# A seven-product Strassen kernel: the sixth product is accumulated into the first PSUM bank

## The chip, the core and the metric

The kernel runs on one core of one Trainium2 chip. The metric is the device time of one execution in microseconds; lower is better. The kernel before takes 2892.92 us, the median of three runs (2892.66 to 2893.03).

## What is computed

The input x has 8 batches, 512 channels and 32 x 32 = 1024 tokens, in fp32. Two attention layers follow each other:

```
layer 0:  xn = layer_norm(x over channels)
          q, k, v = xn Wq', xn Wk', xn Wv'  (+ biases), 8 heads of 64
          out = softmax(q k' / 8) v          per head
          x1  = x + out Wo' + bo
layer 1:  h = group_norm(x1, 32 groups)
          q, k, v = 1x1 projections of h
          p = softmax(q k' / sqrt(512))      one head of 512 channels
          y = x1 + Wp (p v) + bp
```

## The kernel before

The kernel folds the query and key weights of layer 1 into one matrix ("a") and its value and output weights into another ("m"), so layer 1 has a projection qa, scores s, a value projection vm and an output product o. Every product of full matrices is done by a Strassen scheme with seven half-size products instead of eight. The head attention of layer 0 (scores at L805, values at L823) is done directly.

**A unit.** Class `Product` (L325) does one such multiplication for one slice r of the output. `STEPS` (L54) lists its seven products in order: which block or sum of blocks of the left operand, which of the right operand, into which PSUM accumulator (x, y or z), and whether the product opens the accumulator or adds to it. A method `step` (L366) issues the matmuls of one step on TensorE, then pops up to `pieces` entries of side work from a queue (`tick`, L312), then issues what follows on the other engines: a copy of x to SBUF on ScalarE (`copy`, L350, through a function `shift` of the product), or an add of a kept copy and a PSUM bank on VectorE (`out`, L344). Before the change this goes as follows:

| step | product | after it |
|---|---|---|
| 0 | 11 x 11 opens x | copy x to u(0,0) |
| 1 | 12 x 21 opens z | block (0,0) = u(0,0) + z |
| 2 | S2 x T2 adds to x | copy x to u(0,1) |
| 3 | S1 x T1 opens y | nothing |
| 4 | S3 x T3 adds to x | copy x to u(1,1); block (1,1) = u(1,1) + y |
| 5 | 22 x T4 opens z | (q, k, qa and out copy x again with the bias of row block 1); block (1,0) = that copy + z |
| 6 | S4 x 22 adds to y | block (0,1) = u(0,1) + y |

In q, k and qa the copy is an ACTIVATE with a bias (L475), in v, vm, s and o a plain COPY (L458), in the out product a VectorE instruction that adds bias and residual (L901). In s every finished block then gets an exponential in place (L943). In o each finished block is scaled, gets bias and residual, and is stored (L1033 to L1035).

**Where the work stands.** A batch has 18 units: two each (r = 0 and 1) for q, k, v, out, qa, vm and o, four for s; eight batches have 144. The units of most products are issued one after the other: all steps of r = 0, then all of r = 1. In qa, o and each half of s both units do their first two steps before the first does the rest. k of batches 1 to 7 is spread: its first unit stands ahead of the out product, the second is stepped between the parts of the group norm (L1236) and, for its step 6, among the steps of qa (`meanwhile`, L1230).

**PSUM.** `banks_of` (L412) gives the accumulators. y is a bank per unit, from a pool of two. x and z are tiles of two banks (128 x 1024 fp32) from a pool of three; in most products the two units share one tile of each, r choosing the half:

```
            if to == "y":
                return bank(f"y_{tag}_{r}")
            if shared is None or to in own:
                return wide_psum(f"{to}_{tag}_{r}")[:, :HB]
            if to not in shared:
                shared[to] = wide_psum(f"{to}_{tag}")
            return shared[to][:, ts(r, HB)]
```

The out product has an x of its own for each unit (`own="x"`), and k of batches 1 to 7 shares nothing (`apart`).

**Order.** The engines' order is that in which the program issues the instructions (`manual_schedule`, L1089). The tile framework adds the semaphore waits; it finds from the tiles which instruction has to wait for which. SP's queue carries the loads and stores, POOL's queue the folding of row sums.

Of the kernel before, what the change touches and what calls it, by code (L numbers as in the profile page):

```python
# [34 lines left out]
def group_matrix(nc, grp):  # L35
# [21 lines left out]
    ("S2", "T2", "x", False),  # L57
    ("S1", "T1", "y", True),
    ("S3", "T3", "x", False),
    ("22", "T4", "z", True),  # L60
    ("S4", "22", "y", False),
]
BLOCK_OF = {1: (0, 0), 4: (1, 1), 5: (1, 0), 6: (0, 1)}
LOADS_AT = {0: [(0, 0), (0, 1)], 2: [(1, 1)], 3: [(1, 0)]}
SLOTS = ["11", "12", "22", "S1", "S2", "S3", "S4"]


# [1 line left out]
def fast_path(ctx: ExitStack, tc: tile.TileContext, x: bass.AP, vecs: dict, weights: dict, out: bass.AP,  # L69
# [35 lines left out]
    def half_tile(name):  # L105
        return half.tile([P, HB], F32, tag="h", name=name)
# [218 lines left out]
    class Product:  # L325
# [16 lines left out]
            self.done = 0  # L342

        def out(self, i, k, u, ps):  # L344
            if self.in_place and (i, k) != (1, 1):
                self.own[i, k] = u
            nc.vector.tensor_add(self.dest(i, k), u, ps)  # L347
            self.behind.append((i, k))

        def copy(self, which):  # L350
            u = self.loaded.pop(which) if which in self.loaded else half_tile(f"u{which}_{self.tag}")
            self.shift(u, self.x, which)
            return u

        def open(self, to, opens):
            if opens and not hasattr(self, to):
# [9 lines left out]
        def step(self, n=1):  # L366
            for _ in range(n):
                i = self.done
                self.done += 1
                a, b, to, opens = STEPS[i]  # L370
                until(lambda: a in self.a and b in self.b)
                self.open(to, opens)
                if self.ahead:
                    self.ahead(i)
                if i in self.led:
                    self.part(getattr(self, to), self.a[a], self.b[b], opens, (1,))
                elif i == 6 and self.last:
                    next(self.last)
                    return
                else:  # L380
                    self.part(getattr(self, to), self.a[a], self.b[b], opens)
                tick(self.pieces)
                if i == 0:
                    self.u1 = self.copy((0, 0))
                elif i == 1:
                    self.out(0, 0, self.u1, self.z)
                elif i == 2:
                    self.u2 = self.copy((0, 1))
                    if self.last:
                        next(self.last)  # L390
                elif i == 4:
                    u3 = self.copy((1, 1))
                    self.out(1, 1, u3, self.y)
                    self.u3 = u3
                elif i == 5:
                    if self.shift.twice:
                        self.u3 = self.copy((1, 0))
                    self.out(1, 0, self.u3, self.z)
                elif i == 6:
                    self.out(0, 1, self.u2, self.y)  # L400
                if i in (2, 4, 6) or self.at_once:
                    self.finish()

        def finish(self):
# [49 lines left out]
                                 stop=(m == NM // 2 - 1), skip_group_check=True)  # L454
        return part

    def plain_shift():
        return make_shift(lambda u, ps, which: nc.scalar.copy(u, ps))  # L458

    def make_shift(f, twice=False):  # L460
        f.twice = twice
        return f

    def project(tag, w, bias, h, apart=False):

        res, shared = {}, None if apart else {}

        def unit(r):
            def dest(i, k):
                if (i, k) not in res:  # L470
                    res[i, k] = block(f"{tag}_{i}{k}")
                return res[i, k][:, r, :]

            def shift(u, ps, which):
                nc.scalar.activation(u, ps, AF.Identity, bias=bias(2 * which[0] + r))  # L475

            return Product(f"{tag}_{r}", w, h, channel_part(r), make_shift(shift, True), dest,
                           banks_of(tag, r, shared))
        return [unit(r) for r in range(2)], res

    def project_v(tag, w, h):


        res, shared = {}, {}

        def unit(r):
            def dest(i, k):
                if (i, k) not in res:
                    res[i, k] = big_tile(f"{tag}_{i}{k}")
                return res[i, k][:, ts(r, HB)]  # L490

            return Product(f"{tag}_{r}", w, h, token_part(r), plain_shift(), dest, banks_of(tag, r, shared))
        return [unit(r) for r in range(2)], res

    def value_of(v, m, col, width):
# [384 lines left out]
    def project_out(b, w, ot, stats):  # L880

        x1 = {(i, k): block(f"x1_{b}_{i}{k}") for k in range(NH) for i in range(2)}
        shared = {}

        def unit(r):
            def dest(i, k):
                return x1[i, k][:, r, :]

            def load(which):
                i, k = which  # L890
                xr = u.loaded[which] = half_tile(f"xr_{b}_{k}_{2 * i + r}")
                nc.sync.dma_start(out=xr, in_=x[b, ts(2 * i + r, P), ts(k, HB)])

            def ahead(n):
                for which in LOADS_AT.get(n, []):
                    if which not in u.loaded:
                        load(which)

            def shift(t, ps, which):
                oc = 2 * which[0] + r  # L900
                nc.vector.scalar_tensor_tensor(t, ps, bo[:, oc : oc + 1], t, ALU.add, ALU.add)  # L901

            def after(i, k):
                later(lambda: nc.vector.bn_stats(stats[:, 2 * i + r, k, :], dest(i, k)))

            u = Product(f"out_{b}_{r}", w, ot, channel_part(r), make_shift(shift, True), dest,
                        banks_of(f"out_{b}", r, shared, own="x"), after)
            u.ahead = ahead
            load((0, 0))
            return u  # L910
        return [unit(r) for r in range(2)], x1


    class Whole:
# [14 lines left out]
        def scores(self):  # L929
            b = self.b  # L930
            shared = [{}, {}]

            def unit(r):
                g = r // 2

                def dest(i, k):
                    p = self.p[f"{k + 1}{i + 1}"]
                    if p[g] is None:
                        p[g] = block(f"p1_{b}_{k}{i}_{g}")
                    return p[g][:, r % 2, :]  # L940

                def after(i, k):
                    nc.scalar.activation(dest(i, k), dest(i, k), AF.Exp, scale=float(C) ** -0.5)  # L943

                return Product(f"s1_{b}_{r}", self.q, self.hb, key_part(r), plain_shift(), dest,
                               banks_of(f"s1_{b}_{g}", r % 2, shared[g]), after)

            return [unit(r) for r in range(4)]
# [62 lines left out]
        def values(self, v):  # L1011
# [4 lines left out]
            def unit(r):  # L1016
                y, xr_of = {}, {}

                def dest(i, k):
                    if (i, k) not in y:  # L1020
                        y[i, k] = half_tile(f"y_{b}_{r}_{i}{k}")
                    return y[i, k]
# [8 lines left out]
                def after(i, k):  # L1031
# [2 lines left out]
                    nc.vector.scalar_tensor_tensor(t, t, bm[:, oc : oc + 1], xr, ALU.add, ALU.add)  # L1034
                    nc.sync.dma_start(out=out[b, ts(oc, P), ts(k, HB)], in_=t)  # L1035

                u = Product(f"o1_{b}_{r}", w, self.p, value_part(r), plain_shift(), dest,
                            banks_of(f"o1_{b}", r, shared), after)
                def halves(u):


                    a, b_, to, opens = STEPS[6]
                    oc = r
                    xr = half_tile(f"x1r_{b}_last")
                    nc.sync.dma_start(out=xr, in_=self.x1[0, 1][:, ts(r, HB)])
                    nc.vector.tensor_mul(u.u2, u.u2, self.rden[:, ts(1, HB)])
                    nc.vector.scalar_tensor_tensor(xr, u.u2, bm[:, oc : oc + 1], xr, ALU.add, ALU.add)
                    t = dest(0, 1)
                    yield
                    both = (slice(0, HB // 2), slice(HB // 2, HB))  # L1050
                    for cols in both:
                        for m in range(NM // 2):
                            nc.tensor.matmul(u.y[:, cols], w[a][:, m, ts(r, P)],
                                             self.p[b_][m // 2][:, m % 2, cols], start=False,
                                             stop=(m == NM // 2 - 1), skip_group_check=True)
                    for cols in both:
                        queries = slice(HB + cols.start, HB + cols.stop)
                        nc.vector.tensor_mul(t[:, cols], u.y[:, cols], self.rden[:, queries])
                        nc.vector.tensor_add(t[:, cols], t[:, cols], xr[:, cols])
                        nc.sync.dma_start(out=out[b, ts(oc, P), queries], in_=t[:, cols])  # L1060
                    yield

                u.at_once = u.in_place = True
# [621 lines left out]
```

## Time and profile before

One profiled execution stands beside the three timed runs. The lines that the prediction quotes are not repeated here.

| what | value |
|---|---|
| median of three runs | 2892.92 us (2892.66 to 2893.03) |
| span of the profiled execution, first to last instruction | 2891.4 us; its time as a run is not recorded apart |
| median less span | 1.5 us |
| mean granted TensorE clock | 0.999 of full |
| ACTIVATE or COPY of x to SBUF, 128 x 512 | 687 ns (q, k, qa), 586 ns (v, vm, s, o) |
| add of a copy and a bank on VectorE, 128 x 512 | 684 to 689 ns |
| HBM traffic over the span | 79 GB/s |

How to read the rows: a timeline row has the start in us from the span's start, the length in us, engine, line, operation, output tile <- input tiles, shape, and how many instructions are merged in it; in brackets stands the idle time of the engine ahead of it and what ended that. A group row has the count, then busy us and mean ns of one, then idle time ahead and its cause. One fp32 matmul of the program shows as two records. A matmul's record is longer than the distance to the next, since they are pipelined: with 512 columns, 592 ns long and 429 ns apart. The names x_q, y_q, z_q are the accumulators of product q, u(i, k)_q the copies.

### The profile page before, as it was taken

Reading aid. Unit: us, or ns where it says so; the run is one execution under the profiler, and the core shown is the slowest. Engines: PE = TensorE matmul, PEld = TensorE weight load, DVE = VectorE, ACT = ScalarE, POOL = GpSimd, SP = SyncE. Lnnn points to the kernel's source line nnn. Section 1 sums busy time; section 2 is a strip of 40 time slices with the busy share of each in tenths; the row PEclk is TensorE's granted clock in tenths of the full one; section 3 lists DMA queues with packets and bytes.
Section 4 is the critical chain, followed back from the end, with each engine's and each line's share of the span. In section 5 each row is a group of like instructions: output and inputs, shape, how many; then the busy total and the mean of one; then the engine's idle time right before and its main releaser. Section 6 shows DMA issues by size and latency. Waiting matters only on the chain.

```text
span 2891.4 us, 27273 instructions
## 1 busy us (share of the span) xinstructions
PE 2875.6 (99%) x9695; PEld 1379.4 (48%) x9695; DVE 1790.3 (62%) x2325; ACT 1057.9 (37%) x1820; POOL 345.2 (12%) x507
## 2 busy tenths in 40 slices
PE   9999999999999999999999999999999999999999
PEld 4534455345553454534545345543455434553345
DVE  6668465774657655676556755568555685537844
ACT  4462314612256122651225512264222732226331
POOL 2020011200112011120111201011010110002000
PEclk9999999999999999999999999999999999999999
DMA  8134162341623326133252333433244231402302
GB/s 316 46 72 139 37 157 78 68 142 38 181 47 73 135 54 172 43 74 131 62 164 49 84 116 74 152 69 78 102 110 141 61 106 56 124 30 61 118 8 67
DMA packets 110129, 277.17 MB, mean 96 GB/s; under 512 B 16304, under 2 KB 20704, under 8 KB 109984
## 3 DMA queue, kind: packets, MB, share of 16 engines
q1 hardware_dynamic: 81760, 204.51, 20.3%
q0 software_dynamic: 28128, 70.81, 13.3%
q8 instruction: 78, 1.28, 0.2%
q14 instruction: 67, 0.55, 0.1%
q10 hardware_dynamic: 96, 0.02, 0.0%
HBM read 168.85 MB, written 59.24 MB: 79 GB/s over the span
## 4 chain that ended last, share of the span: by engine, by line
PE 97%; DVE 2%; ACT 0%; DMA 0%; issue 0%; DVEq 0%; SPq 0%; ACTq 0%
PE s L805 15%; PE acc L823 15%; PE x_o L453 6%; PE x_s L445 6%; PE y_s L445 4%; PE z_s L445 4%; PE z_o L453 4%; PE y_o L453 4%; PE x_v L437 3%; PE x_vm L437 3%; PE x_q L428 3%; PE x_qa L428 3%; PE x_out L428 3%; PE x_k L428 3%; PE y_q L428 2%; PE y_v L437 2%
## 5 line engine op out<-in xcount | busy, mean ns | idle before, releaser
L814 DVE TENSOR_TENSOR sum<-sum,p 128x1024 f32<-128x1024 f32 x384 | 470.4, 1225 | 40.1 <-DVE sum L814 1.4
L808 ACT ACTIVATE p<-s 128x1024 f32<-128x1024 f32 (+1 forms) x608 | 478.8, 984 | 42.7 <-PE s L805 42.7
L823 PE MATMUL acc<-p,v 128*64 128x512 f32 x2048 | 446.7, 594 | 0.0
L805 PE MATMUL s<-q,k_again 64*128 64x512 f32 x1792 | 392.1, 592 | 0.0
L823 PEld LDWEIGHTS acc<-p,v 128*64 128x64 f32 x2048 | 144.1, 137 | 298.6 <-issue 272.4
L805 PEld LDWEIGHTS s<-q,k_again 64*128 64x128 f32 x1792 | 170.7, 186 | 217.6 <-issue 136.0
L530 POOL DMA_DIRECT2D sum<-sum x78 | 64.0, 823 | 1722.3 <-PE z_vm L437 869.6
L526 POOL DMA_DIRECT2D fold<-sum x312 | 208.6, 755 | 329.4 <-DMA sum<-sum 201.4
L812 DVE TENSOR_TENSOR sum<-p,p 128x1024 f32<-128x1024 f32 x64 | 78.3, 1223 | 179.9 <-ACT p L808 179.9
L445 PE MATMUL x_s<-S_qa,T_gn 128*128 128x512 f32 x256 | 120.3, 592 | 0.0
L827 ACT COPY o<-acc 128x512 f32<-128x512 f32 x63 | 36.9, 586 | 220.0 <-PE acc L823 219.8
L453 PE MATMUL x_o<-T_p,S_vm 128*128 128x512 f32 x256 | 115.2, 592 | 0.0
L943 ACT ACTIVATE p<-p 128x512 f32<-128x512 f32 x128 | 80.7, 630 | 73.1 <-DVE p L347 73.0
L347 DVE TENSOR_TENSOR p<-u(1, 1)_s,y_s 128x512 f32<-128x512 f32 x32 | 22.0, 689 | 132.3 <-ACT u(1, 1)_s L458 132.3
L475 ACT ACTIVATE u(0, 0)_k<-x_k,vecs 128x512 f32<-128x512 f32 x16 | 11.0, 687 | 211.9 <-PE x_k L428 211.9
L869 ACT COPY rr<-r 32x16 f32<-32x16 f32 x256 | 52.6, 205 | 69.4 <-DVE r L772 66.1
L445 PEld LDWEIGHTS x_s<-S_qa,T_gn 128*128 128x128 f32 x256 | 48.6, 190 | 61.2 <-issue 61.0
L453 PEld LDWEIGHTS x_o<-T_p,S_vm 128*128 128x128 f32 x256 | 48.6, 190 | 60.8 <-issue 59.3
L347 DVE TENSOR_TENSOR y<-u(1, 1)_o,y_o 128x512 f32<-128x512 f32 x16 | 11.0, 687 | 99.0 <-ACT u(1, 1)_o L458 99.0
L901 DVE SCALAR_TENSOR_TENSOR xr<-x_out,bo,xr 128x512 f32<-128x512 f32 x64 | 47.7, 745 | 38.4 <-PE x_out L428 38.4
L520 DVE STREAM_TRANSPOSE rden<-rr 128x512 f32<-128x512 f32 (+1 forms) x72 | 53.3, 759 | 26.5 <-ACT rr L869 13.4
L347 DVE TENSOR_TENSOR qa<-u(1, 1)_qa,y_qa 128x512 f32<-128x512 f32 x16 | 11.0, 687 | 81.0 <-ACT u(1, 1)_qa L475 81.0
(353 smaller groups left out, 4589.3 us busy)
## 6 DMA issues: line engine op xcount, KB each, us to landing
sum<-sum POOLq DMA_DIRECT2D x78, 256.0 KB, 3.4
fold<-sum POOLq DMA_DIRECT2D x312, 64.0 KB, 2.4
x<-in_x_dram SPq DMA_DIRECT2D x32, 512.0 KB, 9.0
xr<-in_x_dram SPq DMA_DIRECT2D x64, 256.0 KB, 3.0
x_away<-x SPq DMA_DIRECT2D x32, 512.0 KB
x1r<-x_away SPq DMA_DIRECT2D x63, 256.0 KB, 3.3
k_away<-k SPq DMA_DIRECT2D x28, 512.0 KB, 2.6
k_again<-k_away SPq DMA_DIRECT2D x28, 512.0 KB, 5.5
```

The lines of the kernel that those rows point to most:

```text
L428: nc.tensor.matmul(dst, a[:, k, ts(r, P)], b[:, k, :], start=(opens and k == 0), stop=(k == 1), skip_group_check=True)
L437: nc.tensor.matmul(dst[:, ts(m, CB)], b[:, k, ts(2 * r + m, P)], a[:, k, :], start=(opens and m == 0 and k == 0), stop=(k == 1), skip_grou ...
L445: nc.tensor.matmul(dst, b[:, k, ts(r, P)], a[:, k, :], start=(opens and k == 0), stop=(k == 1), skip_group_check=True)
L453: nc.tensor.matmul(dst, a[:, m, ts(r, P)], b[m // 2][:, m % 2, :], start=(opens and m == 0), stop=(m == NM // 2 - 1), skip_group_check=True)
L526: nc.gpsimd.dma_start(out=f[ts(q + i, BL), :], in_=t[ts(n, BL), ts(i, HB)], accum_op=ALU.add if n else ALU.bypass)
L530: nc.gpsimd.dma_start(out=t[:D, :], in_=t[D:, :], accum_op=ALU.add)
L805: nc.tensor.matmul(parts[i], self.k[m // 4][r, ts(m % 4, P)], self.q[r, :], start=True, stop=True)
L808: nc.scalar.activation(dst, src, AF.Exp, scale=1.0 / float(D) ** 0.5)
L812: nc.vector.tensor_add(self.sum, self.p[0], p)
L814: nc.vector.tensor_add(self.sum, self.sum, p)
L823: nc.tensor.matmul(acc[i * D : (i + 1) * D, :], value_of(self.vt, m, self.c * P + i * D, D), self.p[m][:, ts(i, HB)], start=(m == 0), stop ...
L943: nc.scalar.activation(dest(i, k), dest(i, k), AF.Exp, scale=float(C) ** -0.5)
```

## The change

The sixth and seventh products change places, and 22 x T4 is added to x instead of opening z a second time. x then holds all of block (1,0) when the last step ends, and a single copy takes it out of PSUM: an ACTIVATE with bias in q, k and qa, a COPY in v, vm and o, an exponential straight from PSUM in s, and the bias-and-residual instruction in out. Block (1,1) is now made from a copy of y after step 3 and x after step 4. The loads of residuals follow the new order of blocks.

```diff
 STEPS:
     ("S2", "T2", "x", False),
     ("S1", "T1", "y", True),
     ("S3", "T3", "x", False),
-    ("22", "T4", "z", True),
     ("S4", "22", "y", False),
+    ("22", "T4", "x", False),
 ]
-BLOCK_OF = {1: (0, 0), 4: (1, 1), 5: (1, 0), 6: (0, 1)}
-LOADS_AT = {0: [(0, 0), (0, 1)], 2: [(1, 1)], 3: [(1, 0)]}
+BLOCK_OF = {1: (0, 0), 4: (1, 1), 5: (0, 1), 6: (1, 0)}
+LOADS_AT = {0: [(0, 0), (0, 1)], 1: [(1, 1)], 4: [(1, 0)]}
...
+        def whole(self, i, k):
+            if self.in_place:
+                self.own[i, k] = self.copy((i, k), self.x)
+            else:
+                self.shift(self.dest(i, k), self.x, (i, k), self.loaded.pop((i, k), None))
+            self.behind.append((i, k))
...
                 if i == 0:
-                    self.u1 = self.copy((0, 0))
+                    self.u1 = self.copy((0, 0), self.x)
                 elif i == 1:
                     self.out(0, 0, self.u1, self.z)
                 elif i == 2:
-                    self.u2 = self.copy((0, 1))
+                    self.u2 = self.copy((0, 1), self.x)
+                elif i == 3:
+                    self.u4 = self.copy((1, 1), self.y)
+                elif i == 4:
+                    self.out(1, 1, self.u4, self.x)
+                elif i == 5:
+                    self.finish()
+                    self.out(0, 1, self.u2, self.y)
                     if self.last:
                         next(self.last)
-                elif i == 4:
-                    u3 = self.copy((1, 1))
-                    self.out(1, 1, u3, self.y)
-                    self.u3 = u3
-                elif i == 5:
-                    if self.shift.twice:
-                        self.u3 = self.copy((1, 0))
-                    self.out(1, 0, self.u3, self.z)
                 elif i == 6:
-                    self.out(0, 1, self.u2, self.y)
-                if i in (2, 4, 6) or self.at_once:
+                    self.whole(1, 0)
+                if i in (2, 6) or self.at_once:
                     self.finish()
...
 scores of layer 1:
+                def exponential(p, s):
+                    nc.scalar.activation(p, s, AF.Exp, scale=float(C) ** -0.5)
+
                 def after(i, k):
-                    nc.scalar.activation(dest(i, k), dest(i, k), AF.Exp, scale=float(C) ** -0.5)
+                    if (i, k) != (1, 0):
+                        exponential(dest(i, k), dest(i, k))
+
+                def shift(u, ps, which, add=None):
+                    if which == (1, 0):
+                        exponential(u, ps)
+                    else:
+                        nc.scalar.copy(u, ps)
...
 last step of the last unit:
-                    oc = r
+                    oc = 2 + r
                     xr = half_tile(f"x1r_{b}_last")
-                    nc.sync.dma_start(out=xr, in_=self.x1[0, 1][:, ts(r, HB)])
-                    nc.vector.tensor_mul(u.u2, u.u2, self.rden[:, ts(1, HB)])
-                    nc.vector.scalar_tensor_tensor(xr, u.u2, bm[:, oc : oc + 1], xr, ALU.add, ALU.add)
+                    nc.sync.dma_start(out=xr, in_=self.x1[1, 0][:, ts(r, HB)])
+                    nc.vector.tensor_scalar(xr, xr, bm[:, oc : oc + 1], None, ALU.add)
```

Counted over the program, VectorE has 144 tensor-tensor instructions fewer (1628 to 1484) in the part that normally runs, ScalarE 47 copies more (743 to 790), and TensorE has the same number of matmuls (4872).

More of the change, by code (lines that the diff above doesn't have):

```diff
@@ L344, in out @@
         def out(self, i, k, u, ps):
-            if self.in_place and (i, k) != (1, 1):
+            if self.in_place:
                 self.own[i, k] = u
@@ L348, in out, with copy @@
             self.behind.append((i, k))
-        def copy(self, which):
+        def copy(self, which, ps):
             u = self.loaded.pop(which) if which in self.loaded else half_tile(f"u{which}_{self.tag}")
-            self.shift(u, self.x, which)
+            self.shift(u, ps, which)
             return u
+        def whole(self, i, k):
+            if self.in_place:
+                self.own[i, k] = self.copy((i, k), self.x)
+            else:
+                self.shift(self.dest(i, k), self.x, (i, k), self.loaded.pop((i, k), None))
+            self.behind.append((i, k))
         def open(self, to, opens):
@@ L455, in value_part, with plain_shift @@
         return part
[L457 to L462, printed above, removed]
+    def plain_shift(u, ps, which, add=None):
+        nc.scalar.copy(u, ps)
     def project(tag, w, bias, h, apart=False):
@@ L472, in dest @@
                 return res[i, k][:, r, :]
-            def shift(u, ps, which):
+            def shift(u, ps, which, add=None):
                 nc.scalar.activation(u, ps, AF.Identity, bias=bias(2 * which[0] + r))
-            return Product(f"{tag}_{r}", w, h, channel_part(r), make_shift(shift, True), dest,
+            return Product(f"{tag}_{r}", w, h, channel_part(r), shift, dest,
                            banks_of(tag, r, shared))
@@ L490, in dest @@
                 return res[i, k][:, ts(r, HB)]
-            return Product(f"{tag}_{r}", w, h, token_part(r), plain_shift(), dest, banks_of(tag, r, shared))
+            return Product(f"{tag}_{r}", w, h, token_part(r), plain_shift, dest, banks_of(tag, r, shared))
         return [unit(r) for r in range(2)], res
@@ L897, in ahead, with shift @@
                         load(which)
-            def shift(t, ps, which):
+            def shift(t, ps, which, add=None):
                 oc = 2 * which[0] + r
-                nc.vector.scalar_tensor_tensor(t, ps, bo[:, oc : oc + 1], t, ALU.add, ALU.add)
+                nc.vector.scalar_tensor_tensor(t, ps, bo[:, oc : oc + 1], t if add is None else add, ALU.add, ALU.add)
             def after(i, k):
                 later(lambda: nc.vector.bn_stats(stats[:, 2 * i + r, k, :], dest(i, k)))
-            u = Product(f"out_{b}_{r}", w, ot, channel_part(r), make_shift(shift, True), dest,
+            u = Product(f"out_{b}_{r}", w, ot, channel_part(r), shift, dest,
                         banks_of(f"out_{b}", r, shared, own="x"), after)
@@ L940, in dest, with shift @@
                     return p[g][:, r % 2, :]
+                def exponential(p, s):
+                    nc.scalar.activation(p, s, AF.Exp, scale=float(C) ** -0.5)
                 def after(i, k):
-                    nc.scalar.activation(dest(i, k), dest(i, k), AF.Exp, scale=float(C) ** -0.5)
-                return Product(f"s1_{b}_{r}", self.q, self.hb, key_part(r), plain_shift(), dest,
+                    if (i, k) != (1, 0):
+                        exponential(dest(i, k), dest(i, k))
+                def shift(u, ps, which, add=None):
+                    if which == (1, 0):
+                        exponential(u, ps)
+                    else:
+                        nc.scalar.copy(u, ps)
+                return Product(f"s1_{b}_{r}", self.q, self.hb, key_part(r), shift, dest,
                                banks_of(f"s1_{b}_{g}", r % 2, shared[g]), after)
@@ L1035, in after @@
                     nc.sync.dma_start(out=out[b, ts(oc, P), ts(k, HB)], in_=t)
-                u = Product(f"o1_{b}_{r}", w, self.p, value_part(r), plain_shift(), dest,
+                u = Product(f"o1_{b}_{r}", w, self.p, value_part(r), plain_shift, dest,
                             banks_of(f"o1_{b}", r, shared), after)
@@ L1042, in halves @@
                     a, b_, to, opens = STEPS[6]
-                    oc = r
+                    oc = 2 + r
                     xr = half_tile(f"x1r_{b}_last")
-                    nc.sync.dma_start(out=xr, in_=self.x1[0, 1][:, ts(r, HB)])
-                    nc.vector.tensor_mul(u.u2, u.u2, self.rden[:, ts(1, HB)])
-                    nc.vector.scalar_tensor_tensor(xr, u.u2, bm[:, oc : oc + 1], xr, ALU.add, ALU.add)
-                    t = dest(0, 1)
+                    nc.sync.dma_start(out=xr, in_=self.x1[1, 0][:, ts(r, HB)])
+                    nc.vector.tensor_scalar(xr, xr, bm[:, oc : oc + 1], None, ALU.add)
+                    t = half_tile(f"y_{b}_last")
                     yield
@@ L1052, in halves @@
                         for m in range(NM // 2):
-                            nc.tensor.matmul(u.y[:, cols], w[a][:, m, ts(r, P)],
+                            nc.tensor.matmul(u.x[:, cols], w[a][:, m, ts(r, P)],
                                              self.p[b_][m // 2][:, m % 2, cols], start=False,
@@ L1056, in halves @@
                     for cols in both:
-                        queries = slice(HB + cols.start, HB + cols.stop)
-                        nc.vector.tensor_mul(t[:, cols], u.y[:, cols], self.rden[:, queries])
+                        nc.vector.tensor_mul(t[:, cols], u.x[:, cols], self.rden[:, cols])
                         nc.vector.tensor_add(t[:, cols], t[:, cols], xr[:, cols])
-                        nc.sync.dma_start(out=out[b, ts(oc, P), queries], in_=t[:, cols])
+                        nc.sync.dma_start(out=out[b, ts(oc, P), cols], in_=t[:, cols])
                     yield
```

## The prediction

> **What bounds the kernel now.** I read the busy times and the chain that ended last first (both on the page), then TensorE's own list of waits, then the timeline where one product's first unit gives way to its second.
>
> ```profile
> PE 2875.6 (99%) x9695; PEld 1379.4 (48%) x9695; DVE 1790.3 (62%) x2325; ACT 1057.9 (37%) x1820; POOL 345.2 (12%) x507
> ...
> PE 97%; DVE 2%; ACT 0%; DMA 0%; issue 0%; DVEq 0%; SPq 0%; ACTq 0%
> ```
>
> TensorE is busy for 99% of the span and is 97% of the chain. VectorE, which the change relieves, is at 62% and hardly on it. The list of TensorE's waits shows how little is left to win (columns: engine, tile and line, what it waited for, total us, times, longest):
>
> ```profile
> PE pst_q L263 <- DMA w_q<-in_L_conv_wq_dram: 4.6, 1, 4.6
> PE x_qa L428 <- ACT gn L765: 0.8, 1, 0.8
> PE pm L745 <- DVE mv L739: 0.8, 2, 0.6
> PE z_qa L428 <- DVE qa L347: 0.8, 1, 0.8
> PE y_out L428 <- DVE x L347: 0.6, 1, 0.6
> ```
>
> Apart from the 4.6 us at the start that is some 3 us, nearly all of it in the last batch. So a lighter VectorE can't pay much, and any wait that the change puts on TensorE costs its full length. The place to look is the boundary between two units. This is the timeline there, in batch 1's q product (start us, length us, engine, line, tiles, records merged):
>
> ```profile
> 437.64 1.88 PE L428 MATMUL z_q<-T_h,w_q 128*128 128x512 f32 x4
> 437.84 0.69 ACT L475 ACTIVATE u(1, 1)_q<-x_q,vecs 128x512 f32<-128x512 f32 x1 [1.80 <-PE x_q L428]
> 438.42 0.68 ACT L475 ACTIVATE u(1, 0)_q<-x_q,vecs 128x512 f32<-128x512 f32 x1
> 439.35 1.93 PE L428 MATMUL y_q<-x,w_q 128*128 128x512 f32 x4
> 441.12 1.88 PE L428 MATMUL x_q<-x,w_q 128*128 128x512 f32 x4
> 441.32 0.69 DVE L347 TENSOR_TENSOR q<-u(0, 1)_q,y_q 128x512 f32<-128x512 f32 x1 [0.88 <-PE y_q L428]
> ```
>
> The z row is step 5 of the first unit, the y row step 6, the x row at 441.12 step 0 of the second unit. A step is four records 0.429 us apart, 1.72 us. ScalarE's last reads of x end at 438.42 + 0.68 = 439.10, two microseconds before the second unit writes x: nothing waits. Note when ScalarE reads: it starts 0.20 us after the next step has begun (437.84 - 437.64) and ends 0.89 after it.
>
> **What the Trainium skill says.** *Perfetto Trace Analysis*, "Matmuls": independent groups should rotate through PSUM banks so that the evacuation of one overlaps the matmuls of the next. The trace agrees: y is followed by x with no idle time. *PSUM — Partial Sum Buffer*, "PSUM bank collisions raise a hardware error": guard PSUM by bank and quadrant, so the two units' halves of x (512 fp32 each, a bank each) need no guard against each other. No row here tests that, and it does not help: the wait is in the program. *ScalarE: Activation LUTs*, "What ACT_TABLE_LOAD costs": 186 ns + 0.833 ns per element with immediate scale and bias, some 93 more for a pointer, so 612 and 706 for 512 columns. The trace has 586 (copy), 687 (with bias) and 630 (exponential from SBUF): near enough.
>
> **The change, part by part.**
>
> *VectorE.* Each of 144 units (18 a batch, 8 batches) loses its add for block (1,0): 144 x 0.686 = 99 us of VectorE work. It isn't on the path; worth 0 by itself.
>
> *ScalarE.* q, k, qa keep four copies a unit; v, vm, o (48 units) get a fourth, 48 x 0.586 = 28 us; s keeps three copies and four exponentials. At 37% busy: 0 by itself.
>
> *TensorE.* The same matmuls, two steps swapped. Within a unit the new waits have a step of cover: step 5 reuses y only after step 3's copy of it, step 6 reuses x after step 4's add. Both fit 1.72 us (0.20 + 0.69 from the step's end). S4 is wanted a step earlier, T4 a step later, and the residual loads keep their lead of three steps on SP; the last unit's load stands in SP's queue still ahead of the store of (1,1). Each 0. If that load came late, the tail after the last matmul would grow by up to 1.5 us; the end is otherwise the same multiply, add and store.
>
> *The boundary: an added wait.* In both programs the order of instructions with their waits has a ScalarE wait on the second unit's first touch of x. The halves belong to one tile, so the write of one half waits for the last reader of the other. Before, that reader is the copy after step 4 or 5, long done. Now it is the single copy (or exponential) after step 6, which can't start until the matmul just ahead of the waiting one has ended. Behind that matmul stands all of TensorE. Where x is shared: k of batch 0 (1), q 8, qa 8, v 8, vm 8, o 8, s 16 (two pairs a batch): 57 boundaries. The out product has an x of its own per unit, and so has k of later batches: none there.
>
> The price of one: copy end after the nominal start, plus the restart. The restart is seen in the last batch, where x_qa waits for ScalarE. These two rows, from a window on ScalarE and from one on TensorE,
>
> ```profile
> 2742.01 0.81 ACT L765 ACTIVATE gn<-x,gsh,gsc 128x512 f32<-128x512 f32 x1 [1.21 <-DVE gsh L756]
> ```
> ```profile
> 2742.88 1.13 PE L428 MATMUL x_qa<-gn,w_a 128*128 128x512 f32 x2 [0.78 <-ACT gn L765]
> ```
>
> give 2742.88 - 2742.82, about 0.05 us from copy end to matmul; and the first record after a wait is 697 ns long where others are 592 (minimum and maximum of y_out's records), 0.10 more. So 0.15 us on top. Copy lengths come from the groups of ScalarE kept apart by shape:
>
> ```profile
> L475 ACT ACTIVATE u(0, 0)_q<-x_q,vecs 128x512 f32<-128x512 f32 x16 | 11.0, 687 | 45.1 <-PE x_q L428 45.1
> L458 ACT COPY u(0, 0)_v<-x_v 128x512 f32<-128x512 f32 x16 | 9.4, 586 | 66.1 <-PE x_v L437 66.1
> L943 ACT ACTIVATE p<-p 128x512 f32<-128x512 f32 x128 | 80.7, 630 | 73.1 <-DVE p L347 73.0
> L808 ACT ACTIVATE p<-s 128x512 f32<-128x512 f32 x192 | 116.9, 734 | 0.0
> ```
>
> - q, qa, k: 0.20 + 0.69 + 0.15 = 1.04; 17 of them 17.7 us.
> - v, vm, o: copies start 0.20 to 0.26 after the next step's start, 0.23 + 0.59 + 0.15 = 0.97; 24 of them 23.3 us.
> - s: the exponential from PSUM alone isn't in the trace. Bounds: a copy (0.586) and the row from PSUM with neighbours overlapping (0.734); I take 0.61 (116.9 us busy over 192). 0.23 + 0.61 + 0.15 = 0.99; 16 of them 15.8 us, between 15.5 and 17.8.
>
> *k of later batches.* Its second unit runs beside the group norm. Step 5 now writes y, and waits for step 3's copy, which ScalarE takes only after two scale-and-shift rows of the norm:
>
> ```profile
> 280.01 1.52 ACT L765 ACTIVATE gn<-x,gsh,gsc 128x512 f32<-128x512 f32 x2 [1.21 <-DVE gsh L756]
> 281.43 0.67 ACT L475 ACTIVATE u(1, 1)_k<-x_k,vecs 128x512 f32<-128x512 f32 x1
> ```
>
> The copy in that place ends at 282.10; step 5 (z_k now) starts at 281.17. So 0.93 + 0.15 = 1.08, 7 times 7.6 us.
>
> *What is won.* The 64 records y_out<-o have a mean of 618 ns where 592 is usual: 64 x 26 ns = 1.7 us, one late start in each of 16 steps, a wait for VectorE that only just binds. The y copy now comes a step earlier, and this goes. In the last batch y_out's 0.64 us goes too, as the copy isn't behind the norm's rows on VectorE; the norm's own chain (pm, x_qa, z_qa) is late next, so I take 0.6. Nothing else shrinks.
>
> *Sum.* 17.7 + 23.3 + 15.8 + 7.6 = 64.4, less 2.3: +62.1 us. On the profiled span of 2891.4 that is 2953.5; what lies around it (2892.92 median less 2891.4, 1.5 us) stays: 2955.0, 2.1% slower.
>
> **Rivals.**
> 1. *Cheaper waits.* The k wait is hidden since the norm's rows come earlier (-7.6), or the 0.10 restart isn't paid at 57 boundaries (-5.7). For it: restarts are measured in a few places only. With both 2941.7, with one some 2948. Chance 0.08.
> 2. *Dearer waits.* At q and v boundaries the layer norm's pieces run on ScalarE in between (its square takes 1.05 us); if one stands ahead of the step-6 copy, that boundary pays up to 1.05 more: about half of 16, +8, at most +17: 2963 to 2972. Against: before these copies ScalarE is idle and released by TensorE (1.80 us in the row above). Chance 0.08.
> 3. *Not slower: the boundary does not bind.* If ScalarE's release came before TensorE is ready, only the gain of 2.3 us would stay: 2890.6. That takes the read to end within the 0 us of work between step 6 and the second unit's first write; the point of decision is an independent step (1.72 us) between them, and the instruction order shows none. The relief of VectorE can't repay it: TensorE's waits for VectorE sum to 2.2 us. Chance 0.03.
>
> **How the numbers follow.** The likeliest case, 2955.0 (own range 2949 to 2961), has 0.81. The range, 2946 to 2963, takes in one of the two cheap cases and the near half of the dear one; about 0.15 is outside. A measurement of this kernel can tell about 0.2% (5.8 us) from no change. Slower by more than that: cases 1, 2 and the likeliest, 0.97; within 0.02; faster 0.01.
>
> **What would show it.** In the profile after: TensorE's waits gain rows x_q, x_qa, x_v, x_vm, x_o, x_s <- ACT, 8 times each and 16 for s, 0.7 to 0.8 us idle apiece by the records' own ends (a record ends 0.16 us after the next could start), and y_k <- ACT 7 times; VectorE falls by about 99 us, ScalarE rises by about 28; out shows no boundary wait. I am wrong if TensorE goes from y to the next unit's x without a gap, or if the added time lies in scores or values of the head attention.

## The result and the profile after

| | before | after |
|---|---|---|
| median, us (lowest to highest) | 2892.98 (2892.66 to 2893.19, 4 runs) | 2957.11 (2956.71 to 2957.71, 4 runs) |
| ratio, after to before | | 1.0222 [1.0208, 1.0237] |
| span of the profiled execution, us | 2891.4 | 2954.9 |

The kernel became 64.1 us slower by the medians and 63.5 us by the spans. The forecast was +62.1 us, 2955.0. The time is inside the likeliest case's own range, but two terms of the sum were wrong and hid each other, as the experiments and the reckoning below show.

Three lines of the page of the kernel after: busy time, share of the span and instructions of each engine; then the chain that ended last, by engine.

```profile
PE 2889.6 (98%) x9695; PEld 1384.0 (47%) x9695; DVE 1700.1 (58%) x2181; ACT 1085.0 (37%) x1867; POOL 345.2 (12%) x507
...
PE 88%; DVE 6%; ACT 3%; issue 1%; DMA 1%; DVEq 0%; POOL 0%; ACTq 0%; SPq 0%; POOLq 0%
```

VectorE lost 90 us of work (1790.3 to 1700.1) and the kernel is slower all the same. TensorE has as many instructions as before, but its share of the chain fell from 97% to 88%: the chain now leaves TensorE to pass through other engines. The share doesn't tell where most of the time goes, as experiment 2 shows. Note that TensorE is still "98% busy": that figure alone would not have led anyone to the cause either.

The list of TensorE's waits does (engine, tile and line, what it waited for, total us, times, longest):

```profile
PE x_s L451 <- ACT p L945: 11.0, 16, 0.7
PE y_k L434 <- ACT u(1, 1)_k L477: 10.9, 14, 0.8
PE x_qa L434 <- ACT qa L477: 6.2, 8, 0.8
PE x_q L434 <- ACT q L477: 6.2, 8, 0.8
PE x_o L459 <- ACT u(1, 0)_o L464: 5.4, 8, 0.7
PE x_vm L443 <- ACT vm L464: 5.4, 8, 0.7
PE x_v L443 <- ACT v L464: 5.4, 8, 0.7
PE pst_q L263 <- DMA w_q<-in_L_conv_wq_dram: 4.5, 1, 4.5
...
PE x_k L434 <- ACT k L477: 0.8, 1, 0.8
```

All rows shown but the weight load at the start are new. Apart from y_k each names a product's x bank and a ScalarE copy or exponential, and the counts of these are 16 + 5 x 8 + 1 = 57, the boundaries of the prediction. The out product has no row. The y_k row, a wait inside k's units, has 14 waits where the prediction had 7.

One boundary in full: batch 1's q product, first on TensorE, then on ScalarE (start us, length us, engine, line, tiles).

```profile
448.45 1.88 PE L434 MATMUL x_q<-T_h,w_q 128*128 128x512 f32 x4
451.11 1.98 PE L434 MATMUL x_q<-x,w_q 128*128 128x512 f32 x4 [0.78 <-ACT q L477]
452.93 1.88 PE L434 MATMUL z_q<-x,w_q 128*128 128x512 f32 x4
```
```profile
450.37 0.69 ACT L477 ACTIVATE q<-x_q,vecs 128x512 f32<-128x512 f32 x1 [4.46 <-PE x_q L434]
```

The first TensorE row is step 6, accumulated into x. With four records 0.429 us apart its work would hand over at 448.45 + 1.72 = 450.17. The copy of the finished block starts 0.20 us later and ends at 451.06, and the second unit's first matmul starts at 451.11, 0.94 us late. That unit's first step then takes 452.93 - 451.11 = 1.82 us where 1.72 is usual: 0.10 more for the restart. The list shows only 0.78 for this wait, since a record's printed end (592 ns) lies 0.16 us after the next record could start (429 ns). So the loss at a boundary is the listed idle time + 0.16 + 0.10 (0.163 and 0.105 before rounding).

### The profile page after: what moved, and what is told of

The parts are those of the page before. It is cut to its first block, busy times and chain, and to the rows that moved or that the text cites. A ratio compares the mean times of both kernels' runs of the same rounds, so it can differ in the third digit from the quotient of the medians.

```text
span 2954.9 us, 27325 instructions
## 1 busy us (share of the span) xinstructions
PE 2889.6 (98%) x9695; PEld 1384.0 (47%) x9695; DVE 1700.1 (58%) x2181; ACT 1085.0 (37%) x1867; POOL 345.2 (12%) x507
## 4 chain that ended last, share of the span: by engine, by line
PE 88%; DVE 6%; ACT 3%; issue 1%; DMA 1%; DVEq 0%; POOL 0%; ACTq 0%; SPq 0%; POOLq 0%
PE s L807 12%; PE acc L825 12%; PE x_s L451 8%; PE x_o L459 7%; PE x_v L443 4%; PE x_vm L443 4%; PE x_q L434 4%; PE x_qa L434 4%; PE y_o L459 4%; PE y_s L451 4%; PE x_out L434 4%; DVE sum L816 3%; PE x_k L434 2%; PE y_vm L443 2%; PE y_v L443 2%; PE y_out L434 2%
## 5 line engine op out<-in xcount | busy, mean ns | idle before, releaser
L347 DVE TENSOR_TENSOR p<-u(1, 1)_s,x_s 128x512 f32<-128x512 f32 x32 | 22.0, 688 | 136.5 <-PE x_s L451 136.5
L434 PE MATMUL x_qa<-T_gn,w_a 128*128 128x512 f32 x192 | 91.3, 598 | 6.2 <-ACT qa L477 6.2
L443 PE MATMUL x_vm<-w_m,T_gn 128*128 128x256 f32 x384 | 90.8, 380 | 0.0
L434 PE MATMUL x_out<-T_o,w_o 128*128 128x512 f32 x192 | 89.2, 594 | 0.0
L945 ACT ACTIVATE p<-p 128x512 f32<-128x512 f32 x96 | 60.3, 628 | 60.2 <-DVE p L347 60.2
L459 PEld LDWEIGHTS x_o<-T_p,S_vm 128*128 128x128 f32 x256 | 48.0, 190 | 68.8 <-issue 56.8
L434 PE MATMUL x_k<-T_h,w_k 128*128 128x512 f32 x168 | 79.6, 596 | 0.0
L443 PE MATMUL x_v<-w_v,T_h 128*128 128x256 f32 x336 | 79.4, 380 | 0.0
```

The lines of the kernel that those rows point to most:

```text
L434: nc.tensor.matmul(dst, a[:, k, ts(r, P)], b[:, k, :], start=(opens and k == 0), stop=(k == 1), skip_group_check=True)
L443: nc.tensor.matmul(dst[:, ts(m, CB)], b[:, k, ts(2 * r + m, P)], a[:, k, :], start=(opens and m == 0 and k == 0), stop=(k == 1), skip_grou ...
L459: nc.tensor.matmul(dst, a[:, m, ts(r, P)], b[m // 2][:, m % 2, :], start=(opens and m == 0), stop=(m == NM // 2 - 1), skip_group_check=True)
L945: nc.scalar.activation(p, s, AF.Exp, scale=float(C) ** -0.5)
```

## The experiments

All were run on the chip beside the kernel before, 1 to 4 in one comparison (median of the kernel before 2892.99 us), 5 and 6 in another (2892.87 us). Ratios are to the kernel before. Every kernel computes the whole result; two of them do some work twice or add work that changes nothing.

**1. A tile of its own for each unit's x.** My theory is that the wait comes from the two units' banks of x being one tile. The change is left as it is; only the tile is split.

```diff
-            if shared is None or to in own:
+            if shared is None or to in own or to == "x" and not tag.startswith(f"qa{B - 1}"):
```

The last batch's qa stays shared, so one boundary of 57 is left.

> The changed kernel with one edit: every unit gets an x tile of its own, so that no unit's first write of x waits for another unit's last read (qa of the last batch keeps the shared tile, since the pool has three). Theory (shared x is the cause): 56 of the 57 boundary waits go, at the prices seen in the profile after (0.94 to 1.05 us each, 55.7 us in all); in batches 1 to 7 the second unit of qa now takes the slot of k's x right after its step 6, which puts back 7 waits of 1.05. So 2957.1 - 54.6 + 7.3 = 2909.8 us (2906 to 2913). The 14 waits of k for its y copy stay. Rival A (it is the longer chain of products in one accumulator, or more copies on ScalarE, that costs): x has its matmuls and copies as before, so within 5 us of 2957. Rival B (PSUM slots are short): more tiles make it worse, over 2957.

Measured: 2910.42 us (2909.98 to 2910.60), ratio 1.006 [1.0045, 1.0076]. TensorE's waits in this kernel:

```profile
PE y_k L434 <- ACT u(1, 1)_k L477: 11.1, 14, 1.1
PE x_qa L434 <- ACT k L477: 5.4, 7, 0.8
...
PE x_qa L434 <- ACT gn L767: 0.8, 1, 0.8
PE x_qa L434 <- ACT qa L477: 0.8, 1, 0.8
...
```

The rows x_s, x_q, x_v, x_vm and x_o are gone, and x_qa <- ACT qa is down to one. The kernel is 46.7 us faster than after (47.3 by the start of the last VectorE multiply that waits for TensorE, which leaves the landing of the last stores out). Fifty-six boundaries are removed, worth 54.7 us (57 cost 55.7 us by the table further down, and the one that is left 1.05). In exchange, a second unit of qa now waits 7 times for the copy that ends k's last unit (5.4 us listed, 7 x 1.04 = 7.3 with what the list leaves out). 54.7 - 7.3 = 47.4, close to both. So the boundary's cost is a matter of which tile the next unit writes; neither the single copy itself nor the longer accumulation in x, which are both still there, makes it.

**2. k's y copy put ahead of the pieces on ScalarE's queue.** This concerns the y_k row alone. In k's units the pieces of other work that a step issues come after the copy of y, and the steps that k's second unit takes among the norm's work are spread otherwise.

```diff
-                tick(self.pieces)
+                late = i == 3 and self.tag.startswith("k")
+                if not late:
+                    tick(self.pieces)
...
                     self.u4 = self.copy((1, 1), self.y)
+                    if late:
+                        tick(self.pieces)
...
-                    k_units[1].step((2, 1, 3, 1)[n])
+                    k_units[1].step((2, 3, 2, 0)[n])
```

> The changed kernel with the order of k's work edited: in k the copy of y after step 3 is issued ahead of the side work of that step, and k's second unit does step 4 before the group norm's scale-and-shift rows and steps 5 and 6 after them (2, 3, 2, 0 steps in place of 2, 1, 3, 1). x is shared as in the change. Theory: the 14 waits y_k for ScalarE, 0.94 + 0.10 us each, go: 2957.1 - 14.6 = 2942.5 us (2940 to 2945), and the boundary waits stay as they are. Rival (the k waits are only where an unavoidable delay of TensorE shows): another wait takes their place and the time stays within 3 us of 2957.

Measured: 2942.54 us (2942.00 to 2942.82), ratio 1.0172 [1.0156, 1.0187], 14.6 us less than after. In its list of waits the y_k row is gone and the boundary rows stand as they did:

```profile
PE x_s L455 <- ACT p L949: 11.0, 16, 0.7
PE x_q L438 <- ACT q L481: 6.2, 8, 0.8
```

So the two causes are separate. Fourteen waits of 10.9 / 14 + 0.16 + 0.10 = 1.04 us are 14.6 us, and 14.6 is what went. The edit has two parts, and what each does to the waits was not measured apart.

This also tells what the chain of the result section was worth. Here are its shares in experiment 1, where the 14 waits of k stand and 56 boundary waits are gone, and in experiment 2, where all boundary waits stand and those of k are gone:

```profile
PE 89%; DVE 6%; ACT 2%; issue 1%; DMA 1%; DVEq 0%; POOL 0%; ACTq 0%; SPq 0%; POOLq 0%
```
```profile
PE 98%; ACT 1%; DMA 0%; DVE 0%; issue 0%; SPq 0%; DVEq 0%
```

So the fall to 88% comes nearly all from k's waits. At one of them the chain turns off to work on ScalarE that itself waited for a long run of VectorE sums, and stays away from TensorE for 36 us (at the first of them, from 211.6 to 247.8 us); at a boundary it leaves for one copy. A share of the chain says where the path ran, not what a wait costs.

**3. The read at the boundary made twice as long.** If the time from step 6's end to the end of its reader is what counts, then issuing the copy (or exponential) of block (1,0) a second time must lengthen each boundary by up to one read. The work done twice changes nothing in the result.

```diff
             if self.in_place:
                 self.own[i, k] = self.copy((i, k), self.x)
+                self.shift(self.own[i, k], self.x, (i, k))
             else:
-                self.shift(self.dest(i, k), self.x, (i, k), self.loaded.pop((i, k), None))
+                add = self.loaded.pop((i, k), None)
+                for _ in range(2):
+                    self.shift(self.dest(i, k), self.x, (i, k), add)
```

> The changed kernel with the suspected cost doubled: the copy (or exponential) of x after step 6 is issued twice, into the same place. Theory: at each of 57 boundaries TensorE waits for both, 0.49 to 0.72 us more each (a second row starts 0.58 us after the first with a bias, some 0.1 less as a copy; more if the second waits for the first): 30 to 38 us more, 2991 us (2987 to 2995). Rival (ScalarE's read is covered, the time is lost elsewhere): ScalarE has room at 37%, so within 5 us of 2957.

Measured: 2996.69 us (2995.61 to 2997.33), ratio 1.0358 [1.0342, 1.0374], 39.6 us more than after, and 1.7 us above the range that I expected. Its waits:

```profile
PE x_s L454 <- ACT p L948: 21.1, 16, 1.3
PE x_q L437 <- ACT q L480: 12.0, 8, 1.5
PE x_qa L437 <- ACT qa L480: 12.0, 8, 1.5
PE y_k L437 <- ACT u(1, 1)_k L480: 10.8, 14, 0.8
PE x_v L446 <- ACT v L467: 10.3, 8, 1.3
PE x_vm L446 <- ACT vm L467: 10.3, 8, 1.3
PE x_o L462 <- ACT u(1, 0)_o L467: 10.3, 8, 1.3
...
PE pm L750 <- DVE mv L744: 1.8, 2, 1.4
PE x_k L437 <- ACT k L480: 1.5, 1, 1.5
```

Each boundary row rose and y_k did not. The rise is 10.1 (x_s) + 2 x 5.8 (x_q, x_qa) + 3 x 4.9 (x_v, x_vm, x_o) + 0.7 (x_k) = 37.1 us, or 0.61 to 0.73 us a boundary: the full length of a read (0.60, 0.59, 0.69), with nothing of it hidden. My expectation had the two reads overlap, as two copies in a row did in the kernel before. They don't; this is the pair at a boundary of q:

```profile
455.44 1.41 ACT L480 ACTIVATE q<-x_q,vecs 128x512 f32<-128x512 f32 x2 [4.46 <-PE x_q L437]
```

The 1.2 us of pm, a small product of the group norm, come from the doubled VectorE instruction of the out product. That is 38.3, and the start of the last VectorE multiply that waits for TensorE moved by 2986.98 - 2948.73 = 38.25 us. Of the rest of the 39.6, 1.05 us lies behind that multiply (7.22 us to the end of the span, 6.17 in the kernel after).

**4. Both repairs together.** Edits 1 and 2 on the kernel after.

> Both edits: an x tile per unit and the order of k's work. With k's step 6 ahead of qa the slot of k's x is free in time, so the 7 waits that the first edit alone would put back should not be there. Theory: 56 boundary waits and 14 k waits go: 2957.1 - 54.6 - 14.6 = 2887.9 us (2885 to 2892), some 5 us under the kernel before, since the late starts of step 6 in q, k, qa and out, and one stall of the last batch, are gone as well. Rival (what the change saves is off the path entirely): the same as the kernel before, 2893 within 1.

Measured: 2888.45 us (2886.88 to 2889.65, 21 runs), ratio 0.9984 [0.9978, 0.9991]. This is the fastest version: 68.7 us under the kernel after, and 4.5 us under the kernel before. The difference to before is small, but the interval excludes 1. Its waits, beside those for the weights at the start:

```profile
PE x_qa L438 <- ACT gn L771: 0.8, 1, 0.8
PE x_qa L438 <- ACT qa L481: 0.8, 1, 0.8
PE z_qa L438 <- DVE qa L347: 0.8, 1, 0.8
...
PE pm L751 <- DVE mv L745: 0.6, 1, 0.6
```

The two edits apart took off 46.7 and 14.6, 61.3 together; both at once take 7.4 us more. That matches the 7 waits x_qa <- ACT k of experiment 1 (7.3 us), which are not in this list: in the new order k's last step no longer stands just ahead of qa's second unit.

**5. Edit 1 on the kernel before.** A rival reading of experiment 1 is that separate x tiles are better in any case, so that the kernel before would gain as well.

> The kernel before with the same edit as the first experiment, an x tile per unit (qa of the last batch keeps the shared one). Theory: before the change nothing waits at a boundary, so a tile of its own changes nothing: 2893.0 us within 1. Rival (a tile per unit is itself worth something or costs something, so that the first experiment overstated or understated the guard): a difference of several us, in either direction.

Measured: 2892.73 us (2891.93 to 2893.65, 12 runs), ratio 1.0000 [0.9992, 1.0009]. By itself the split is worth nothing. In this program it pays only where a read stands directly ahead of the next write.

**6. VectorE's load given back.** Where do the 4.5 us of experiment 4 come from: from VectorE's lighter load, or from the earlier copies of y? To the kernel of experiment 4 I added one VectorE instruction on each finished block (1,0), outside k and out. It takes the maximum of the block with itself, which leaves it as it was.

```diff
+            u = self.own[i, k] if self.in_place else self.dest(i, k)
+            if not self.tag.startswith(("k", "out")):
+                nc.vector.tensor_tensor(u, u, u, ALU.max)
```

> The kernel with both edits (x tile per unit, k order), in which VectorE gets back an instruction per unit after step 6 in q, v, qa, s, vm and o: an elementwise maximum of the finished 128 x 512 block with itself, which leaves its values as they are. 112 instructions of some 0.69 us, 77 us of VectorE. Theory (VectorE's relief was worth nothing by itself; the few us under the kernel before come from the earlier copy of y): 2888.4 us within 1.5. Rival (the relief is what made it faster than before): 3 to 5 us slower, back to about 2893.

Measured: 2889.43 us (2888.45 to 2896.15, 21 runs), ratio 0.9989 [0.9983, 0.9996]. The added 112 instructions raised VectorE from 1697.6 to 1770.1 us busy, and the time by 1.0 us (1.1 when each is held against the kernel before of its own comparison); the two intervals overlap, so whether this is more than nothing isn't shown. In the two profiled executions the last multiply starts 1.29 us later, of which some 0.6 is a longer wait for a weight load at the start. Of the 4.5 us under the kernel before, 3.4 stay. So at least three quarters of the gain isn't VectorE's load. That it is the earlier copies of y is argued, from the late starts listed below; no run has these copies without the rest of the change. The added instruction doesn't stand in the place of the old add, nor at all 144 units, so this bounds the effect of load, not of every wait that the old adds caused.

## Why the prediction was right, and where it was not

**The mechanism.** The prediction put the loss in the write of one half of x waiting for the last reader of the other half, with that reader now directly behind step 6. The list of waits shows it at the 57 places named, experiment 1 removes it by splitting the tile, and experiment 3 lengthens it by the length of a read. *PSUM — Partial Sum Buffer*, "PSUM bank collisions raise a hardware error", in the Trainium skill, asks for a guard per bank and quadrant; the halves here are a bank each. The prediction said that no row tested this. Experiment 1 agrees for banks of different tiles: there the copy of one overlaps the matmuls into the other, and of the 57 waits one is left, where the tile is still shared. That two banks of one tile could do the same has no run.

**The price of a boundary.** The terms against what they measured, from the waits in the timeline (0.78, 0.675, 0.69 and 0.777 us on average) with 0.163 + 0.105 = 0.268 added:

| term | predicted | measured |
|---|---|---|
| q, qa, k: 17 | 1.04 each, 17.7 us | 0.78 + 0.268 = 1.048, 17.8 us |
| v, vm, o: 24 | 0.97 each, 23.3 us | 0.675 + 0.268 = 0.943, 22.6 us |
| s: 16 | 0.99 each, 15.8 us | 0.69 + 0.268 = 0.958, 15.3 us |
| k of later batches, y | 7 x 1.08 = 7.6 us | 14 x 1.045 = 14.6 us |
| gains | -2.3 us | -6.2 us (by what is left) |
| sum | +62.1 us | +64.1 us |

The boundaries cost 55.7 us where 56.8 was predicted. The exponential from PSUM, which before did not show by itself, is now a row of ScalarE's groups kept apart by shape:

```profile
L945 ACT ACTIVATE p<-p 128x512 f32<-128x512 f32 x96 | 60.3, 628 | 60.2 <-DVE p L347 60.2
L945 ACT ACTIVATE p<-x_s 128x512 f32<-128x512 f32 x32 | 19.1, 597 | 64.4 <-PE x_s L451 64.4
```

597 ns, against 610 taken in the prediction; the prediction's 612, an estimate from the formula of *ScalarE: Activation LUTs*, "What ACT_TABLE_LOAD costs", is 2 to 3% too long for it. The same function, working in place in SBUF, takes 628.

**The first step that failed: "k of later batches. Its second unit runs beside the group norm."** I looked for work ahead of the y copy in the second unit alone. The first unit has such work too: eight small copies of the softmax's reciprocals. This is ScalarE in the kernel after:

```profile
243.74 0.69 ACT L477 ACTIVATE u(0, 1)_k<-x_k,vecs 128x512 f32<-128x512 f32 x1 [2.75 <-PE x_k L434]
245.38 1.71 ACT L871 COPY rr<-r 32x16 f32<-32x16 f32 x8 [0.96 <-DVE r L774]
247.12 0.69 ACT L477 ACTIVATE u(1, 1)_k<-y_k,vecs 128x512 f32<-128x512 f32 x1
```

and TensorE beside it:

```profile
245.25 1.88 PE L434 MATMUL x_k<-T_h,w_k 128*128 128x512 f32 x4
247.85 1.98 PE L434 MATMUL y_k<-x,w_k 128*128 128x512 f32 x4 [0.73 <-ACT u(1, 1)_k L477]
```

y's copy could have started at about 245.45, when step 3 was done; it starts at 247.12 and ends at 247.81, and the step that writes y again starts at 247.85 where it would have started at 246.97. The same small copies stood in the profile before. There they cost nothing: step 3 had no copy of its own, and the copy of x after step 4, which comes next, still started 0.20 us after that step's end (242.68 + 1.72 = 244.40):

```profile
242.68 1.88 PE L428 MATMUL x_k<-T_h,w_k 128*128 128x512 f32 x4
```
```profile
242.81 1.71 ACT L869 COPY rr<-r 32x16 f32<-32x16 f32 x8 [0.97 <-DVE r L772]
244.59 0.69 ACT L475 ACTIVATE u(1, 1)_k<-x_k,vecs 128x512 f32<-128x512 f32 x1
```

So this could have been read from the profile before. It follows also that "Within a unit the new waits have a step of cover" did not hold for k's first unit: the 0.20 + 0.69 us of a copy fit into a step, the 1.71 us ahead of it did not. Seven further waits cost 7.0 us more; the seven that were predicted, in the second units, cost 1.08 each as predicted (0.81 listed). Experiment 2 confirms the size of both sets together, 14.6.

**The second: "Nothing else shrinks."** Only y_out's late starts were counted. Three rows of TensorE's groups before (mean ns is the second number after the bar):

```profile
L428 PE MATMUL y_out<-o,w_o 128*128 128x512 f32 x64 | 31.7, 618 | 0.6 <-DVE x L347 0.6
L428 PE MATMUL y_qa<-gn,w_a 128*128 128x512 f32 x64 | 30.9, 605 | 0.0
L428 PE MATMUL y_q<-x,w_q 128*128 128x512 f32 x56 | 27.0, 605 | 0.0
```

and after:

```profile
L434 PE MATMUL y_out<-o,w_o 128*128 128x512 f32 x64 | 30.1, 593 | 0.0
L434 PE MATMUL y_qa<-gn,w_a 128*128 128x512 f32 x64 | 30.1, 593 | 0.0
L434 PE MATMUL y_q<-x,w_q 128*128 128x512 f32 x56 | 26.3, 593 | 0.0
```

A mean of 605 ns is one late record of about 50 ns in each step of four, which is easy to pass over. y_out gave 1.6 us and its stall in the last batch 0.6; y_qa and y_q gave 0.8 and 0.7 us. A k group of the same kind (599 ns before) and pm gave some 0.6 together. That is 4.3 of the 6.2 us; the rest I could not locate. In the kernel of experiment 4 the same y_out, y_qa and y_q rows stand at 592 ns, and there the gain shows as time: 4.5 us under the kernel before.

The two failures are +7.0 and -3.9 us, and the boundary prices were off by -1.1. Together they leave the forecast 2.0 us short: good luck as much as good reckoning.

**The rivals.** Cheaper waits fell: the restart is paid (1.82 us for 1.72 in the timeline), and k's wait is there, twice as often. Dearer waits, with a piece of the layer norm ahead of the copy, fell as well: the longest wait in each boundary row is no more than 0.1 us above its mean. "Not slower" fell with the first row of the list. *Engine loads:* summed over its groups, VectorE's instructions fell by 98.6 us, 99 as predicted; the page's 90 counts the time in which two records overlap only once. ScalarE rose by 27, for 28 predicted. As shown above, giving VectorE 72 us of work back moved the time by about 1 us. For ScalarE no run tests it alone, but experiment 4 has the added load and is the fastest.

**The tail.** Predicted unchanged. The last multiply on VectorE waits for TensorE in both programs, and starts at 2884.31 us before and at 2948.73 after; from there to the end of the span are 7.1 and 6.2 us. In the experiments that keep the changed tail it is 6.1 to 7.2, and 6.6 in the kernel of experiment 5, which has the old one: the landing of the last stores varies by a microsecond, and no late residual load added to it. Up to that multiply the loss is 64.4 us.

**What stays open.** Between one and two microseconds of the gain have no row. Whether the wait could go with one shared tile and a finer guard was not tried, as the waits are put in when the program is built.

## What to carry to other kernels

When the last accumulation of one block stands directly ahead of the first of the next and both use the same tile, even in different banks, and the framework guards by tile as here, the whole latency of taking the block out of PSUM (start, read, restart; here 0.94 to 1.05 us) falls on TensorE: count these boundaries, and give each bank a tile of its own before counting saved VectorE adds. When an edit brings a reader of a buffer and its next writer closer together, look through every unit that runs this code for what stands ahead of that reader on its engine, since work that was harmless there before becomes a wait. Here, with TensorE on 97% of the chain, 90 us less on VectorE was worth no more than the late starts of TensorE that went with it. These show as a group's mean a few per cent above its minimum.

## What the runs showed of the hardware

- A wait of TensorE costs more than the list says: 0.16 us because the record's end lies after the next possible start (592 ns long, 429 apart), and 0.10 us in the first record after the wait (697 ns for 592). At the q boundary 0.78 listed is 1.05 lost.
- The exponential of 128 x 512 fp32 takes 597 ns from PSUM into SBUF and 628 ns in place in SBUF. Whether the source or the working in place makes the difference was not tried.
- Two ScalarE reads of one bank in a row don't always overlap. In the kernel before, the two copies of x behind step 4 start 0.58 us apart at 0.69 us each (the timeline of the prediction), in keeping with *ScalarE: Activation LUTs*, "What ACT_TABLE_LOAD costs", by which neighbours overlap by some 93 ns. In experiment 3 the same copy twice into the same block took 1.41 us (its row is shown there), with no overlap. Whether the shared destination is the reason was not tried.
